# First-layer edge sums split around the row maxima, with one block difference per slot

## The chip, the cores and the metric

One core of a Trainium2 chip runs the kernel. The metric is the device time of one execution in microseconds (us), taken as the median of several runs. A core has five engines that run side by side: TensorE (PE, with its weight load PEld), VectorE (DVE), ScalarE (ACT), GpSimd (POOL) and SyncE (SP), which issues the DMA transfers here. Each engine works through its own queue in order and waits on semaphores for the others.

## The reference, cut to what matters

There are two layers; the change is in the first one, a graph attention over 8 batches (B) of 512 tokens with 512 features (F). The second is a normal self-attention with 16 heads and is not touched.

```python
self_feat = concat(x, q) @ W_self.T + b_self            # B x 512 x 512
for d in range(2):                                       # adjacency and its transpose
    A = adj if d == 0 else swapaxes(adj, 1, 2)
    A = A[:, :, :20, :]                                  # 20 neighbours, 11 labels
    cond = A.sum(-1)                                     # sum over the 11 labels
    vb = A @ w_bias + b_bias                             # weighted sum over the labels
    aff = einsum(q_heads, k_heads) / sqrt(dh)
    aff = where(cond > 0, aff, -9e15) + vb
    w = softmax(aff)                                     # over the 20 neighbours
    output += attention(w, kv, Wout) + bout
x = x + relu(output)
```

For each token there are 16 heads x 40 scores (2 directions x 20 neighbours), 640 numbers in a row. The mask and the additive term depend on token and neighbour only: 40 numbers per token, made from 440 integer labels.

## The kernel before, in words

A batch is called a block `b`. It is cut into four pieces `c` of 128 tokens, so the first layer has 32 slots `n` = 4b + c, written out as one Python loop under a manual schedule: the order of the statements in the loop is the order of each engine's queue. In slot n the loop works on several pieces at once:

- `turn_weights(n)` (L561) turns the finished softmax weights on PE, and ACT copies them out (L563).
- `normalize0(n+1)`: ACT takes the exponential (L550), DVE sums it and takes the reciprocal (`den`, L553 and L554), and POOL multiplies by it (L555).
- `scores0(n+2)`: PE makes the scores (`pss`, L529), DVE takes them out of PSUM (L533) and POOL multiplies by the mask (L535).
- `add_edges(n+2)`: POOL adds the additive term (L539).
- `self_feat_product`: PE makes a later block's features by a seven-product scheme for 2x2 quarters (L356). Per block, the slots c = 0 to 3 carry the products (4, 5), (3), (1, 2) and (6, 7); DVE or ACT takes them out, and DVE adds the collected ones at the slot's end (`TO_ADD0`, L692: none at c = 0 and 1, one at c = 2, three at c = 3).
- `result0(n)`: PE makes the output piece (`po`, L571 and L573), DVE finishes it (L574) and SP stores it.
- `less_top(n+2)`: DVE takes the row maxima (`top`, L546) and POOL subtracts them (L547).
- `edges(b+1+c//2, (c+2)%4)`: DVE makes one piece of a later block's mask and additive term in five instructions. These are a plain sum of the labels (L257), the comparison with zero that gives the mask (L258), a product with the label weights (L259), its sum (L260), and the bias (L261).
- At c = 0, DVE makes the small `lt` (L292) for a later block; PE turns it in the next slot (`pl`, L298).
- At c = 1, `far_away(b+1)` on POOL turns the mask into 0 or -9e15 (L266) and adds it to the additive term (L267).
- At c = 1, SP also issues 20 small loads of `vo` (L516) and the two 440 KB label loads of block b+2 (L246), and before them the 1 MB load of the turned features `vt` of block b+3 (L218).
- `turned_sums(b+2, i)`: POOL makes the four quarter differences of the turned features that the products read (L342): differences 2 and 0 at c = 0, 1 at c = 1, 3 at c = 2, none at c = 3.

Some slots carry more: slots 0 and 1 the sums of the self weights (L335, DVE), slot 8 the gate vectors (L584 on DVE, `pg` on PE), slots 10 to 13 the keys of the second half on PE, and slots 15 to 18, 22 and 23 statistics and norms of the second layer's first block (L93, L111 on DVE). From slot 26 on there are no edges, differences or products. After the loop the second layer follows.

Label tiles and `vt` tiles have two buffers each, and the mask and additive tiles two each.

Of the kernel before, what the change touches and what calls it, by code (L numbers as in the profile page):

```python
# [9 lines left out]
F32 = mybir.dt.float32  # L10
# [3 lines left out]
ALU = mybir.AluOpType  # L14
AX = mybir.AxisListType
# [3 lines left out]
B, N, F = 8, 512, 512  # L19
P = 128  # L20
# [5 lines left out]
D2 = 2 * NG  # L26
# [5 lines left out]
BIG = 9000000000000000.0  # L32
# [12 lines left out]
def graph_then_self_attention(ctx: ExitStack, tc: tile.TileContext, x, x_t, near, near_t, labels, w_self_t, wq, wk_t,  # L45
                              wout_t, wg_t, wb_t, wqkv_t, wp_t, cols, gate_vecs, rows, out):
    nc = tc.nc

    def blocks(ap):
        return ap.rearrange("(c p) f -> p c f", p=P)  # L50
# [118 lines left out]
    def quarter(t, p, q):  # L169

        return t[:, 2 * p:2 * p + 2, M * q:M * (q + 1)]


    with ExitStack() as l0:
        w0 = l0.enter_context(tc.tile_pool(name="w0", bufs=1))
        two = l0.enter_context(tc.tile_pool(name="two", bufs=2))
# [32 lines left out]
        def load_x(b):  # L209
            X[b] = xp.tile([P, C, F], F32, tag="x", name=f"x_{b}")  # L210
            nc.sync.dma_start(X[b], blocks(x[b]))
# [3 lines left out]
        def load_vt(b):  # L215
            VT[b] = turned.tile([P, C, N], F32, tag="turned", name=f"vt_{b}")
            for cut in (slice(0, 2), slice(2, C)) if b == 0 else (slice(0, C),):
                nc.sync.dma_start(VT[b][:, cut], blocks(x_t[b])[:, cut])  # L218
# [21 lines left out]

        MASK, ADD, LABELS = {}, {}, {}

        def load_labels(b):
            for i in range(2):
                LABELS[b, i] = two.tile([P, 2, D2 * L], I32, tag="labels", name=f"labels_{b}_{i}")
                nc.sync.dma_start(LABELS[b, i], labels[b, i * N // 2:(i + 1) * N // 2, :].rearrange("(c p) m -> p c m", p=P))  # L246

        def edges(b, c):


            if c == 0:
                MASK[b] = two.tile([P, C, D2], F32, tag="mask", name=f"mask_{b}")
                ADD[b] = two.tile([P, C, D2], F32, tag="add", name=f"add_{b}")
            src = LABELS[b, c // 2][:, c % 2, :].rearrange("p (m l) -> p m l", l=L)
            weighted = src.bitcast(F32)
            total = two.tile([P, D2], F32, tag="total", name=f"total_{b}_{c}")
            nc.vector.tensor_reduce(total, src, AX.X, ALU.add)  # L257
            nc.vector.tensor_scalar(MASK[b][:, c, :], total, 0.0, None, ALU.is_gt)  # L258
            nc.vector.tensor_tensor(weighted, src, edge_bc[:, None, 0:L].to_broadcast([P, D2, L]), ALU.mult)  # L259
            nc.vector.tensor_reduce(total, weighted, AX.X, ALU.add)  # L260
            nc.vector.tensor_scalar(ADD[b][:, c, :], total, edge_bc[:, L:L + 1], None, ALU.add)  # L261

        def far_away(b):

            far = two.tile([P, C, D2], F32, tag="far", bufs=1, name=f"far_{b}")
            nc.gpsimd.tensor_scalar(far, MASK[b], 1.0, BIG, ALU.subtract, ALU.mult)  # L266
            nc.gpsimd.tensor_tensor(ADD[b], ADD[b], far, ALU.add)  # L267

        vo = w0.tile([P, 2, KB, P], F32, name="vo")
        nc.gpsimd.memset(vo, 0.0)  # L270
# [48 lines left out]
        def self_feat(b, blocks_of_f):  # L319

            self_feat_rest(b, self_feat_main(b, blocks_of_f))
# [15 lines left out]
        def turned_sums(b, n):  # L337

            B11, B12, B21, B22 = (quarter(VT[b], p, q) for p in range(2) for q in range(2))
            TB[n] = {0: B12, 3: B21}.get(n) or parts.tile([P, 2, M], F32, tag=f"t{n}", name=f"ts{n + 1}_{b}")  # L340
            x0, x1 = ((B12, B11), (B22, TB.get(0)), (B22, B12), (B21, TB.get(1)))[n]
            nc.gpsimd.tensor_tensor(TB[n], x0, x1, ALU.subtract)  # L342
# [195 lines left out]
        def add_edges(b, c, engine=nc.gpsimd):  # L538
            engine.tensor_tensor(T[b, c], T[b, c], ADD[b][:, c, None].to_broadcast([P, H, D2]), ALU.add)  # L539
# [9 lines left out]
        def normalize0(b, c):  # L549
            nc.scalar.activation(T[b, c], T[b, c], AF.Exp)  # L550
            tv = T[b, c].rearrange("p h (d m) -> p (h d) m", d=2)
            den = three.tile([P, 2 * H, 1], F32, tag="den", name=f"den_{b}_{c}")
            nc.vector.tensor_reduce(den, tv, AX.X, ALU.add)  # L553
            nc.vector.reciprocal(den, den)  # L554
            nc.gpsimd.tensor_tensor(tv, tv, den.to_broadcast([P, 2 * H, NG]), ALU.mult)  # L555

        def turn_weights(b, c):
            flat = T[b, c].rearrange("p h e -> p (h e)")
            pt = pair(f"ptw_{b}_{c}").rearrange("p a n -> p (a n)")
            for i in range(KB):  # L560
                nc.tensor.transpose(pt[:, i * P:(i + 1) * P], flat[:, i * P:(i + 1) * P], ident)  # L561
            wt = two.tile([P, KB, P], F32, tag="wt", name=f"wt_{b}_{c}")
            nc.scalar.copy(wt, pt[:, :KB * P].rearrange("p (i n) -> p i n", i=KB))  # L563
            WT[b, c] = wt
# [33 lines left out]
        for n in range(2 * C):  # L598
            d, f = n % 2, n // 2
# [20 lines left out]
        live_of(1)  # L620
        self_feat(1, (0, 1))
        load_vt(2)
        for n, (b, c) in enumerate(slots):
            turn_weights(b, c)

            if n + 3 == len(slots):
                scores0(*slots[n + 2])
            if n + 1 < len(slots):
                normalize0(*slots[n + 1])
            if n + 3 < len(slots):  # L630
                scores0(*slots[n + 2])
            if n + 2 < len(slots):
                add_edges(*slots[n + 2], nc.vector if n + 3 == len(slots) else nc.gpsimd)
            if n < 2:
                self_feat(1, (c + 2,))
            elif b + 1 + c // 2 < B:
                for i in ((4, 5), (3,), (1, 2), (6, 7))[c]:
                    self_feat_product(b + 1 + c // 2, i)
            if 26 <= n < len(slots) - 2:
                less_top(*slots[n + 2])  # L640
            if c == 1 and b + 2 < B:
                live_of(b + 2)
                if b + 3 < B:
                    load_vt(b + 3)
            if n in (10, 11, 12, 13):
                keys(1, n - 10, 0)
            if n in (24, 25):
                for f in (2 * (n - 24), 2 * (n - 24) + 1):
                    turn(0, f)
            group = {26: lambda: q_or_k(0, 0), 27: lambda: q_or_k(1, 0), 29: lambda: value(0), 30: lambda: value(1),  # L650
                     31: lambda: value(2)}.get(n, lambda: None)()
            if group:
                group.half(0)
                if n < 30:
                    group.half(1)
            if n == 10:
                gate_columns(gb)
            result0(b, c)
            if n >= 30:
                group.half(1)  # L660
            if n < 26:
                less_top(*slots[n + 2])
            if n in (10, 11, 12, 13):
                keys(1, n - 10, 1)
            if b + 1 + c // 2 < B:
                edges(b + 1 + c // 2, (c + 2) % 4)
            if c == 0 and b + 2 < B:
                live_sums(b + 2)
            if c == 1:
                if b + 1 < B:  # L670
                    far_away(b + 1)
                    load_vo(b + 1)
                if b + 2 < B:
                    load_labels(b + 2)
            if c == 2 and b + 2 < B:
                q_row(b + 2)
            if c == C - 1 and b + 3 < B:
                load_x(b + 3)
            if n == 4:
                WG = [weight("wg", wg_t), weight("wb", wb_t)]  # L680
            if n == 8:
                gb = gate_vectors()
                WQ.update({(d, 1): weight(f"wq{d}_1", wq[d]) for d in range(2)})

            if n < 2:
                for i in ((0, 1), (3, 2))[n]:
                    weight_sums0(i)
            if b + 2 < B:
                for i in ((2, 0), (1,), (3,), ())[c]:
                    turned_sums(b + 2, i)  # L690
            for sf, y in TO_ADD0:
                nc.vector.tensor_tensor(sf, y, sf, ALU.add)  # L692
            TO_ADD0.clear()

            if n in (17, 18, 19, 24):
                i = min(n - 17, 3)
                W1.append(weight(f"w1_{i}", (*(wqkv_t[i] for i in range(3)), wp_t)[i]))
            if n in (23, 28):
                fetch((n - 23) // 5)
            if n == 9:  # L700
                early = weight("early", mid[0])
            if 15 <= n < 19:
                norm_stats(0, n - 15, early)
            for i in {22: (0, 1), 23: (2, 3)}.get(n, ()):
                norm(0, i, early)
# [334 lines left out]
    with tc.manual_schedule():  # L1040
# [22 lines left out]
        for n, (b, g, c) in enumerate(steps):  # L1063
# [41 lines left out]
            if at in OUTPUT_SUMS_AT:  # L1105
                back, i = OUTPUT_SUMS_AT[at]
# [94 lines left out]
```

## Time and profile before

| what | value |
|---|---|
| median of 3 runs | 1327.74 us (1327.66 to 1327.84) |
| the profiled execution's own time | 1324.78 us |
| its span in the profile | 1323.0 us |
| granted TensorE clock | 0.999 |
| PE, DVE, ACT, POOL busy | 98%, 72%, 54%, 64% |
| first layer's loop of slots | about 66 us to 407 us of the span |

The profiled execution is 2.96 us (0.2%) below the median of the runs, and 1.78 us of it lie outside the span. Lines of the trace have the start in us, the duration, the engine, the line of the kernel (L555), the operation, output and inputs, and in brackets how long the engine had stood idle and what ended the wait. PE is shown as busy nearly everywhere because the ends of its pipelined matmuls are modelled, so its waits are read better from its weight loads.

### The profile page before, as it was taken

Reading aid. Unit: us, or ns where it says so; the run is one execution under the profiler, and the core shown is the slowest. Engines: PE = TensorE matmul, PEld = TensorE weight load, DVE = VectorE, ACT = ScalarE, POOL = GpSimd, SP = SyncE. Lnnn points to the kernel's source line nnn. Section 1 sums busy time; section 2 is a strip of 40 time slices with the busy share of each in tenths; the row PEclk is TensorE's granted clock in tenths of the full one; section 3 lists DMA queues with packets and bytes.
Section 4 is the critical chain, followed back from the end, with each engine's and each line's share of the span. In section 5 each row is a group of like instructions: output and inputs, shape, how many; then the busy total and the mean of one; then the engine's idle time right before and its main releaser. Section 6 shows DMA issues by size and latency. Waiting matters only on the chain.

```text
span 1323.0 us, 29745 instructions
## 1 busy us (share of the span) xinstructions
PE 1298.1 (98%) x11347; PEld 988.7 (75%) x11347; DVE 958.4 (72%) x1759; ACT 708.8 (54%) x1740; POOL 841.5 (64%) x921
## 2 busy tenths in 40 slices
PE   9999999999999999999999999999999999999997
PEld 6567777877765687777777777777777777777776
DVE  4467787777855668687768768776785876776887
ACT  2333233323225665766666666666567567566664
POOL 0066775677563546677577667756866774775776
PEclk9999999999999999999999999999999999999999
DMA  9523552343212000001002000100200010010010
GB/s 346 175 96 110 177 191 83 111 159 135 90 58 80 1 2 1 2 18 64 2 2 78 5 1 17 65 1 1 81 2 1 18 65 1 2 49 2 10 41 33
DMA packets 46492, 78.66 MB, mean 59 GB/s; under 512 B 9680, under 2 KB 14224, under 8 KB 46352
## 3 DMA queue, kind: packets, MB, share of 16 engines
q1 hardware_dynamic: 45920, 76.22, 16.7%
q8 instruction: 91, 1.49, 0.5%
q10 hardware_dynamic: 432, 0.55, 0.1%
q14 instruction: 49, 0.40, 0.1%
HBM read 59.27 MB, written 17.49 MB: 58 GB/s over the span
## 4 chain that ended last, share of the span: by engine, by line
PE 74%; DVE 13%; POOL 8%; issue 3%; ACT 1%; DMA 0%; POOLq 0%; DVEq 0%; ACTq 0%
PE pst L786 18%; PE pt L942 16%; PE s L917 9%; PE pao L957 8%; PE psp L829 6%; PE pss L529 3%; POOL t L535 3%; POOL t L539 3%; PE psf_p L356 2%; PE pqk L138 1%; DVE top L924 1%; DVE top L546 1%; DVE mask L258 1%; PE pz L124 1%; DVE den L553 1%
## 5 line engine op out<-in xcount | busy, mean ns | idle before, releaser
L937 POOL TENSOR_SCALAR e<-e,den 128x512 f32<-128x512 f32 x511 | 361.8, 708 | 267.1 <-DVE den L934 172.7
L929 ACT ACTIVATE e<-s,top 128x512 f32<-128x512 f32 x512 | 348.5, 697 | 131.5 <-DVE top L924 131.5
L924 DVE TENSOR_REDUCE top<-s 128x2 f32<-128x1024 f32 x256 | 301.0, 1217 | 18.6 <-PE s L917 17.2
L942 PEld LDWEIGHTS pt<-ident,e 128*128 128x128 f32 x2048 | 234.5, 141 | 82.4 <-POOL e L937 25.2
L942 PE MATMUL pt<-ident,e 128*128 128x128 f32 x2048 | 289.8, 276 | 3.2 <-ACT et L944 1.6
L944 ACT COPY et<-pt 128x512 f32<-128x512 f32 x369 | 209.3, 596 | 101.5 <-PE pt L942 100.7
L917 PE MATMUL s<-k_pair,q_pair 32*128 32x512 f32 x992 | 143.7, 640 | 0.0
L529 PE MATMUL pss<-kq,sf 128*128 128x320 f32 x512 | 142.9, 433 | 0.0
L957 PEld LDWEIGHTS pao<-et,v 128*32 128x32 f32 x4096 | 107.5, 110 | 44.4 <-issue 44.4
L957 PE MATMUL pao<-et,v 128*32 128x128 f32 x4096 | 126.5, 274 | 0.0
L529 PEld LDWEIGHTS pss<-kq,sf 128*128 128x128 f32 x512 | 95.0, 190 | 36.1 <-ACT kq L486 0.3
L929 ACT ACTIVATION_READ_ACCUMULATOR e<-s,top 128x1 f32 x512 | 109.2, 213 | 0.0
L944 DVE COPY et<-pt 128x512 f32<-128x512 f32 x143 | 96.3, 673 | 3.4 <-PE pt L942 2.8
L555 POOL TENSOR_TENSOR t<-t,den 128x640 f32<-128x640 f32 x32 | 40.7, 1272 | 59.6 <-DVE den L554 54.0
L550 ACT ACTIVATE t<-t 128x640 f32<-128x640 f32 x32 | 23.6, 738 | 94.0 <-POOL t L547 93.9
L535 POOL TENSOR_TENSOR t<-t,mask 128x640 f32<-128x640 f32 x32 | 49.4, 1544 | 31.2 <-issue 30.3
L546 DVE TENSOR_REDUCE top<-t 128x32 f32<-128x640 f32 x32 | 26.2, 818 | 56.3 <-POOL t L539 56.3
L547 POOL TENSOR_TENSOR t<-t,top 128x640 f32<-128x640 f32 x32 | 40.7, 1271 | 34.0 <-DVE top L546 34.0
L126 ACT ACTIVATE ht<-pz,gates_t 128x512 f32<-128x512 f32 x32 | 24.7, 777 | 64.6 <-PE pz L124 64.6
L563 ACT COPY wt<-ptw 128x640 f32<-128x640 f32 x32 | 22.2, 693 | 67.4 <-PE ptw L561 67.3
L917 PEld LDWEIGHTS s<-k_pair,q_pair 32*128 32x128 f32 x992 | 41.0, 183 | 20.8 <-issue 17.3
L786 PE MATMUL pst<-t,w 128*128 128x256 f32 x224 | 53.7, 383 | 0.0
(272 smaller groups left out, 2276.3 us busy)
## 6 DMA issues: line engine op xcount, KB each, us to landing
x<-in_x SPq DMA_DIRECT2D x8, 1024.0 KB
mid<-x SPq DMA_DIRECT2D x32, 256.0 KB
xq<-mid SPq DMA_DIRECT2D x8, 1024.0 KB
out<-o SPq DMA_DIRECT2D x31, 256.0 KB
vt<-in_x_t SPq DMA_DIRECT2D x7, 1024.0 KB
labels<-in_labels SPq DMA_DIRECT2D x16, 440.0 KB
wq<-in_wq SPq DMA_DIRECT2D x4, 1024.0 KB
gate<-gates SPq DMA_DIRECT2D x8, 512.0 KB
```

Of the source, the lines that this page charges most:

```text
L529: nc.tensor.matmul(o, SF[b][:, k, cut], KQ[b][:, k, on], start=(k == 0), stop=(k == C - 1))
L535: nc.gpsimd.tensor_tensor(t, t, MASK[b][:, c, None].to_broadcast([P, H, D2]), ALU.mult)
L547: nc.gpsimd.tensor_tensor(tv, tv, top.to_broadcast([P, 2 * H, NG]), ALU.subtract)
L786: nc.tensor.matmul(out[:, m, :], fixed[:, k, m * P:(m + 1) * P], moving[:, k, :], start=(k == 0), stop=(k == 1))
L829: nc.tensor.matmul(out[:, m, :], t[:, k, m * P:(m + 1) * P], a[:, k, :], start=(k == 0), stop=(k == 1))
L917: nc.tensor.matmul(S[n][j // 2][:, j % 2, :], Q[b, g][on, c * P:(c + 1) * P], K[b, g][on, :], start=True, stop=True)
L924: nc.vector.tensor_reduce(TOP[n][:, 2 * pair:2 * pair + 2], S[n][pair], AX.X, ALU.max, negate=True)
L929: nc.scalar.activation(e, S[n][pair][:, j % 2, :], AF.Exp, bias=TOP[n][:, j:j + 1], accum_out=DEN[n][:, j:j + 1])
L937: engine.tensor_scalar(E[n][j], E[n][j], DEN[n][:, j:j + 1], att_scale, ALU.mult, ALU.mult)
L942: nc.tensor.transpose(pt[:, k * P:(k + 1) * P], E[n][j][:, k * P:(k + 1) * P], ident)
L944: copy(et, pt.rearrange("p (k n) -> p k n", k=C))
L957: nc.tensor.matmul(PAO[b, g][DH * j:DH * (j + 1), at], V[b][:, k, DH * h:DH * (h + 1)], ET[n, j][:, k, :], start=(k == 0), stop=(k == C - 1))
```

## The change

`edges` gets a third argument. Its first half (label sum and mask) is now issued before `less_top` of the same slot, its second half (weighted sum and bias) after it. Before the loop, both halves of the first pieces still run together. `far_away` is on DVE instead of POOL. Each slot has one difference of turned features: 0, 1 and 3 at c = 0, 1, 2, and at c = 3 difference 2 of block b+3; one more (`turned_sums(2, 2)`) runs ahead of the loop. The first label load of block b+2 is issued at c = 0, the second stays at c = 1.

```diff
-        def load_labels(b):
-            for i in range(2):
+        def load_labels(b, halves=(0, 1)):
+            for i in halves:
...
-        def edges(b, c):
+        def edges(b, c, halves=(0, 1)):
...
+            if 0 in halves:
+                nc.vector.tensor_reduce(total, src, AX.X, ALU.add)
+                nc.vector.tensor_scalar(MASK[b][:, c, :], total, 0.0, None, ALU.is_gt)
+            if 1 not in halves:
+                return
             nc.vector.tensor_tensor(weighted, src, edge_bc[:, None, 0:L].to_broadcast([P, D2, L]), ALU.mult)
...
         def far_away(b):
...
-            nc.gpsimd.tensor_scalar(far, MASK[b], 1.0, BIG, ALU.subtract, ALU.mult)
-            nc.gpsimd.tensor_tensor(ADD[b], ADD[b], far, ALU.add)
+            nc.vector.tensor_scalar(far, MASK[b], 1.0, BIG, ALU.subtract, ALU.mult)
+            nc.vector.tensor_tensor(ADD[b], ADD[b], far, ALU.add)
...
         load_vt(2)
+        turned_sums(2, 2)
         for n, (b, c) in enumerate(slots):
...
+            if b + 1 + c // 2 < B:
+                edges(b + 1 + c // 2, (c + 2) % 4, (0,))
             if n < 26:
                 less_top(*slots[n + 2])
...
             if b + 1 + c // 2 < B:
-                edges(b + 1 + c // 2, (c + 2) % 4)
+                edges(b + 1 + c // 2, (c + 2) % 4, (1,))
...
                 if b + 2 < B:
-                    load_labels(b + 2)
+                    load_labels(b + 2, (1,))
+            if c == 0 and b + 2 < B:
+                load_labels(b + 2, (0,))
...
-            if b + 2 < B:
-                for i in ((2, 0), (1,), (3,), ())[c]:
-                    turned_sums(b + 2, i)
+            if b + 2 + c // 3 < B:
+                turned_sums(b + 2 + c // 3, (0, 1, 3, 2)[c])
```

More of the change, by code (lines that the diff above doesn't have):

```diff
@@ L241, in graph_then_self_attention @@
         MASK, ADD, LABELS = {}, {}, {}
-        def load_labels(b):
-            for i in range(2):
+        def load_labels(b, halves=(0, 1)):
+            for i in halves:
                 LABELS[b, i] = two.tile([P, 2, D2 * L], I32, tag="labels", name=f"labels_{b}_{i}")
                 nc.sync.dma_start(LABELS[b, i], labels[b, i * N // 2:(i + 1) * N // 2, :].rearrange("(c p) m -> p c m", p=P))
-        def edges(b, c):
-            if c == 0:
+        def edges(b, c, halves=(0, 1)):
+            if c == 0 and 0 in halves:
                 MASK[b] = two.tile([P, C, D2], F32, tag="mask", name=f"mask_{b}")
@@ L255, in edges @@
             weighted = src.bitcast(F32)
-            total = two.tile([P, D2], F32, tag="total", name=f"total_{b}_{c}")
-            nc.vector.tensor_reduce(total, src, AX.X, ALU.add)
-            nc.vector.tensor_scalar(MASK[b][:, c, :], total, 0.0, None, ALU.is_gt)
+            total = two.tile([P, D2], F32, tag="total", name=f"total_{b}_{c}_{halves[0]}")
+            if 0 in halves:
[3 more added lines that the diff above has]
+                return
             nc.vector.tensor_tensor(weighted, src, edge_bc[:, None, 0:L].to_broadcast([P, D2, L]), ALU.mult)
```

## The prediction

> **What bounds the kernel now.** I read the page's chain first: it tells which engine's work ended last, over the whole span.
>
> ```profile
> ## 4 chain that ended last, share of the span: by engine, by line
> PE 74%; DVE 13%; POOL 8%; issue 3%; ACT 1%; DMA 0%; POOLq 0%; DVEq 0%; ACTq 0%
> ```
>
> PE bounds most of it, but 21% is DVE and POOL. The chain in order of time puts those into the first layer's loop of slots (66 to 407 us), the stage that the change touches. So next comes the view of the line that opens each slot on PE, the turning of the weights.
>
> ```profile
> L561 PEld LDWEIGHTS ptw<-ident,t x160: 138/140/145, 76.6 to 401.4; 128*128 128x128 f32 x160
> ...
> its engine sat idle before it (us, times) until:
>   POOL t L555: 22.9, 27
> ```
>
> PE's weight load waits 22.9 us for POOL's product with `den` (L555). About a quarter us of each of the 27 waits is the modelled end of the matmul before. Comparing each slot's opening with the end of its predecessor's output (L573), what PE really loses is 8.0 us in slots 2 to 9 and 7.4 us in slots 16 to 25. Slots 10 to 15 have none: the second keys fill PE. These 15.4 us are about the most that the change can win.
>
> What L555 waits for is seen in the timeline of one slot (c = 0, slot 20), from one L555 to the next:
>
> ```profile
> 305.40 1.27 POOL L555 TENSOR_TENSOR t<-t,den 128x640 f32<-128x640 f32 x1 [4.55 <-DVE den L554]
> ...
> 308.26 1.54 POOL L539 TENSOR_TENSOR t<-t,add 128x640 f32<-128x640 f32 x1
> ...
> 309.83 0.82 DVE L546 TENSOR_REDUCE top<-t 128x32 f32<-128x640 f32 x1 [1.45 <-POOL t L539]
> 310.57 0.60 DVE L257 TENSOR_REDUCE total<-labels 128x40 f32<-128x440 int32 x1
> 310.74 1.27 POOL L547 TENSOR_TENSOR t<-t,top 128x640 f32<-128x640 f32 x1 [0.94 <-DVE top L546]
> 311.21 0.84 DVE L258 TENSOR_SCALAR mask<-total 128x40 f32<-128x40 f32 x1
> ...
> 311.97 1.74 POOL L342 TENSOR_TENSOR ts<-vt 128x512 f32<-128x512 f32 x1
> 311.97 0.60 DVE L259 TENSOR_TENSOR labels<-labels,vec 128x440 f32<-128x440 int32 x1
> 312.04 0.74 ACT L550 ACTIVATE t<-t 128x640 f32<-128x640 f32 x1 [3.76 <-POOL t L547]
> 312.60 0.61 DVE L260 TENSOR_REDUCE total<-labels 128x40 f32<-128x440 f32 x1
> 313.25 0.49 DVE L261 TENSOR_SCALAR add<-total,vec 128x40 f32<-128x40 f32 x1
> ...
> 313.73 0.80 DVE L553 TENSOR_REDUCE den<-t 128x32 f32<-128x640 f32 x1
> ...
> 315.07 1.27 POOL L555 TENSOR_TENSOR t<-t,den 128x640 f32<-128x640 f32 x1
> ```
>
> The reader sees a ring: L555, L535, L539, then `top` 4.43 us after L555's start, L547, the exponential (done at 312.78), `den`, and 1.34 us later L555 again. `den` could have started at about 312.8; it started at 313.73, because DVE was at the edges. With no edges the ring takes 8.74 us (slot 26). Also, DVE stood idle for 1.45 us just before `top`.
>
> Two rows behave oddly. L258 takes 0.84 us here and 0.18 at its shortest, and it ends as POOL's L547 ends (312.01 against 312.05). L342 takes 1.74 us beside L259, and 1.27 elsewhere. Such DVE and POOL instructions exclude each other. Who goes first is seen at slot 1:
>
> ```profile
> 103.64 0.68 DVE L335 TENSOR_TENSOR s_self<-ws,s_self 128x512 f32<-128x512 f32 x1
> 103.88 0.83 POOL L267 TENSOR_TENSOR add<-add,far 128x160 f32<-128x160 f32 x1 [0.47 <-DVE add L261]
> 104.24 1.02 DVE L335 TENSOR_TENSOR ws<-ws 128x512 f32<-128x512 f32 x1
> ```
>
> L267 (0.52 alone) waits for the first L335, goes before the second, and the second ends 0.34 us late. A waiting POOL instruction gets in between two products of DVE.
>
> **The change part by part.** Times are from `top`'s start (T), in the order of DVE's queue.
>
> *First half before `top`.* L257 and L258 leave the ring: 0.60 us, and 0.76 from L258's start to L259's. They go where DVE idled. L574 at 307.71, L257 until 308.9; L258 then waits for POOL's L539 and ends with it (0.04 us later, as after L547), when `top` may start anyway. Cost 0. If PE is the bound, DVE comes late from `po` and the cover is gone: `top` is then 1.35 us after the end of `po` instead of 0.65. So POOL may run ahead of PE by about 1.4 us, no more.
>
> *Second half after `top`.* L259 now starts at T+0.74, before L547 (T+0.90). L547 is held up. Row first: L259 holds POOL off for 0.46 us of its 0.60 (slot 12: L259 at 223.65, L342 at 223.76 took 1.62, 0.35 over 1.27). So L547 runs T+1.20 to 2.47, +0.30 us on the ring. The Trainium skill ("SBUF — State Buffer", section "Who interferes with whom") states a rule against this change: a DVE operation with two SBUF inputs, and a GpSimd operation that reads SBUF, take a shared port pair for the whole instruction, and the later one fully blocks. By the rule's whole 0.60 us, L547 would start at T+1.34: +0.44. That would be 0.14 us more in each of some 18 slots, 2.5 us in all; I take the row. L261 ends with L547, at T+2.5. The exponential ends at T+3.24, `den` can start, and L555 comes at T+4.60.
>
> *c = 0.* `lt` follows L261; its product on POOL comes after. Interval from L555 to L555: 4.43 + 4.60 = 9.03 us (before: 9.66). PE's 0.43 us wait for `lt` in the next slot goes too.
>
> *c = 1.* POOL loses 1.04 + 0.52 us; it was the bound here (9.94). DVE gains L266 and L267. No row shows these on DVE. The first, by L258 (40 columns, 0.18) and L111 (512 columns, 0.50): 0.26 us. The second, by L259 (440 columns, 0.60) and L335 (512, 0.68): about 0.30. Below nothing neither can be; above, each can wait for POOL's 1.27 us L342. The first follows L261 directly, as L259 follows L258, and gets in; the second needs the first's result, and in that gap the waiting L342 goes (as L267 between the L335s): T+2.75 to 4.0. The second ends at T+4.3, L555 is at T+5.6: 10.05 us. With no such wait it is 9.05.
>
> *c = 2.* L692 gets in after L261 (until T+3.0), L342 after it: 9.03 us (before 10.18).
>
> *c = 3.* Three L692 (0.60 apart), and new beside them L342. The first goes, L342 takes T+3.0 to 4.3, the others end at T+5.4: 11.18 us (before 11.14, where POOL was free). Alone they would end at T+4.3: 10.1.
>
> *What costs nothing.* The difference ahead of the loop: POOL stands idle for 6.12 us until 83.70, and `vt`, issued at 65.92, is in by about 73 (the DMA share falls to 0 from 74 us). It can delay the edges there by about 0.4 us, which slot 1's PE (bound by itself) covers. `far_away(0)` meets 2.88 us of DVE idle before 38.5. At c = 3 the new L342 reads a `vt` issued two slots earlier, with 5 us to land, and overwrites what product 7 read some 5 us before. Queues: on SP the first label load (0.4 us of issue) now stands before `vt` and the 20 `vo` issues, `vt` waits there for PE anyway; the second stays behind `vo`. Labels have at least a slot and a half to land.
>
> **The sum.** One undisturbed block before (L555 at 127.84 to 168.76) is 9.94 + 10.18 + 11.14 + 9.66 = 40.92 us. After, 39.29. PE's own need is 9.85 us for a slot with two products (233.31 to 243.12 and on), about 9.0 with one: 38.6. So the ring still binds, at c = 1 and c = 3.
>
> I walk the slots: PE opens at the later of its own need and L555 + 1.33. Slot 3 opens at 107.5 (107.85 before), 6 at 136.8 (138.82), 9 at 168.2 (170.84), 10 at 177.9 (181.60). The keys keep that 3.7 us. At slot 17 it is 3.3, since POOL's lead is capped; then 301.6 for slot 21 (306.73) and 343.9 for slot 25 (349.66). In slots 15 to 18 the statistics add 1.03 us behind the edges, and in 22 a norm waits behind L342. The gain is 5.7 us, and afterwards PE carries it to the end. The profiled execution (1324.78) would be 1319.1. The median was 2.96 higher; the same off it is 1322.0.
>
> **The rivals.**
>
> *PE becomes the bound (22%).* If DVE keeps the pair through its row of instructions at c = 1 and 3, intervals are 9.03, 9.05, 9.03, 10.1 = 37.2, under PE's 38.6. For it: L259 after L258 beats L342 every time. Against: the L335 rows. Slot 10 opens 5.8 us earlier, slots 14 to 25 bring 7.7: 13.5, so 1314.2.
>
> *POOL wins every contest (8%), slower.* If L342 takes the pair at L547's end before L261, DVE stands until T+3.8 in each slot: 9.7 + 10.1 + 10.2 + 11.45 = 41.45, 0.5 us a block over four and a half blocks, plus 0.7 at the statistics of c = 1: about 3 us, 1330.7. It decides where L261 is longer than 1.5 us. Against: in all the slots before, L258 waiting behind L547 went ahead of L342.
>
> *It is given back (12%).* The lead cap or another DVE tail takes the 0.5 to 1 us a slot back, and PE's waits move to `po` or products: 1326 to 1328. For it: a quarter of the ring's freed time already goes to L547.
>
> **How the numbers follow.** My forecast has 58%, and its own range is 1319 to 1324.7 (the 2.5 us of the rule, the two contests each way). With the others: 80% faster, 12% within 0.2% (2.7 us, about what a measurement of this kernel can tell from no change), 8% slower. The range 1315 to 1327 leaves out the fastest end and the slower case.
>
> **What would show it.** Right: L258 ends with L539 and `top` does not move from L555 + 4.43; L547 starts 1.2 us after `top`; L555's wait of PE falls from 22.9 to about 17 us; c = 2 drops to 9.0; at c = 3 an L692 of about 1.3 us more. Wrong: `top` later than 4.6 us after L555 outside the keys' slots, L261 over 1.5 us, POOL waiting for `vt`, or PE waiting for products.

## The result and the profile after

The changed kernel takes 1318.0 us (median of 4 runs, 1315.49 to 1318.51), the kernel before, run beside it, 1327.7. The ratio is 0.9926, with a 95% interval of 0.9909 to 0.9943: it is faster by 0.7%, or 9.7 us. The profiled execution took 1315.49 us with a span of 1313.7, 9.3 us less than the one before, at the same granted clock of 0.999.

The page's chain shows where DVE and POOL have gone: their 21% have become 10%, and PE's 74% have become 87%.

```profile
## 4 chain that ended last, share of the span: by engine, by line
PE 87%; DVE 8%; POOL 2%; issue 1%; ACT 1%; DMA 0%; POOLq 0%; DVEq 0%; ACTq 0%
```

The line that opens each slot on PE (L561 before, L564 now) waits 9.3 us instead of 22.9 for POOL's product with `den` (L558 now), and 17 times instead of 27:

```profile
L564 PEld LDWEIGHTS ptw<-ident,t x160: 138/141/144, 76.2 to 391.3; 128*128 128x128 f32 x160
...
its engine sat idle before it (us, times) until:
  POOL t L558: 9.3, 17
```

The timeline of slot 20 (c = 0), from one L558 to the next, is the counterpart of the one shown before. Lines have moved: L258 and L259 are the label sum and mask, L262 to L264 the second half, L549 the maxima, L550 their subtraction.

```profile
297.36 1.27 POOL L558 TENSOR_TENSOR t<-t,den 128x640 f32<-128x640 f32 x1 [2.41 <-DVE den L557]
...
300.22 1.54 POOL L542 TENSOR_TENSOR t<-t,add 128x640 f32<-128x640 f32 x1
300.26 0.60 DVE L258 TENSOR_REDUCE total<-labels 128x40 f32<-128x440 int32 x1
300.90 0.90 DVE L259 TENSOR_SCALAR mask<-total 128x40 f32<-128x40 f32 x1
301.79 0.82 DVE L549 TENSOR_REDUCE top<-t 128x32 f32<-128x640 f32 x1
302.53 0.61 DVE L262 TENSOR_TENSOR labels<-labels,vec 128x440 f32<-128x440 int32 x1
302.69 1.58 POOL L550 TENSOR_TENSOR t<-t,top 128x640 f32<-128x640 f32 x1 [0.93 <-DVE top L549]
303.17 0.61 DVE L263 TENSOR_REDUCE total<-labels 128x40 f32<-128x440 f32 x1
303.81 0.49 DVE L264 TENSOR_SCALAR add<-total,vec 128x40 f32<-128x40 f32 x1
304.22 0.16 DVE L295 TENSOR_SCALAR lt<-sums 128x4 f32<-128x4 f32 x1
304.23 1.29 POOL L345 TENSOR_TENSOR vt<-vt 128x512 f32<-128x512 f32 x1
304.30 0.74 ACT L553 ACTIVATE t<-t 128x640 f32<-128x640 f32 x1 [4.06 <-POOL t L550]
305.07 0.82 DVE L556 TENSOR_REDUCE den<-t 128x32 f32<-128x640 f32 x1 [0.69 <-ACT t L553]
...
306.42 1.27 POOL L558 TENSOR_TENSOR t<-t,den 128x640 f32<-128x640 f32 x1 [0.91 <-DVE den L557]
```

The mask, held up by POOL's addition, ends with it (301.80 against 301.76), and the maxima start 4.43 us after L558 as before. The subtraction (L550) starts 0.90 us after the maxima as before and takes 1.58 us instead of 1.27: what the prediction had as a later start shows in the profile as a longer instruction. `den` now waits for ACT, where it used to wait for DVE's row of edge work: 0.69 us of DVE idle stand before it. The interval is 9.06 us instead of 9.67.

Intervals from one POOL product with `den` to the next, by the c of the slot that they start in (slots 4 to 7 of before and after; PE's own need is 9.8 us for a slot with two products and 8.5 for one with one):

| c | before | predicted | measured |
|---|---|---|---|
| 0 | 9.66 | 9.03 | 9.07 |
| 1 | 9.94 | 10.05 | 9.66 |
| 2 | 10.18 | 9.03 | 9.06 |
| 3 | 11.14 | 11.18 | 11.08 |
| sum | 40.92 | 39.29 | 38.87 |

The contests of c = 1 and c = 3, in which DVE and POOL want to run instructions that exclude each other, are seen in the timeline: first slot 21, then slot 19, and last slot 19 of the kernel before. L269 and L270 are the large number on DVE, L699 (L692 before) the collected sums, L345 POOL's difference:

```profile
312.88 0.49 DVE L264 TENSOR_SCALAR add<-total,vec 128x40 f32<-128x40 f32 x1
313.29 0.23 DVE L269 TENSOR_SCALAR far<-mask 128x160 f32<-128x160 f32 x1
313.29 1.36 POOL L345 TENSOR_TENSOR ts<-vt 128x512 f32<-128x512 f32 x1
313.36 0.74 ACT L553 ACTIVATE t<-t 128x640 f32<-128x640 f32 x1 [4.07 <-POOL t L550]
313.55 1.28 DVE L270 TENSOR_TENSOR add<-add,far 128x160 f32<-128x160 f32 x1
...
314.75 0.81 DVE L556 TENSOR_REDUCE den<-t 128x32 f32<-128x640 f32 x1
```

```profile
293.14 2.96 DVE L699 TENSOR_TENSOR sf<-ys,sf 128x512 f32<-128x512 f32 x3
293.14 1.80 POOL L345 TENSOR_TENSOR ts<-vt 128x512 f32<-128x512 f32 x1
```

```profile
302.25 1.89 DVE L692 TENSOR_TENSOR sf<-ys,sf 128x512 f32<-128x512 f32 x3
```

L270 takes 1.28 us, and 0.33 where POOL is free (its minimum is 0.326): it ends 0.18 us after L345 (314.83 against 314.65). The three L699 take 2.96 us instead of 1.89, and L345 1.80 instead of 1.27, as one L699 goes before it and two after it.

### The profile page after: what moved, and what is told of

It is laid out like the page before. It is cut to its first block, busy times and chain, and to the rows that moved or that the text cites. A ratio compares the mean times of both kernels' runs of the same rounds, so it can differ in the third digit from the quotient of the medians.

```text
span 1313.7 us, 29713 instructions
## 1 busy us (share of the span) xinstructions
PE 1295.4 (99%) x11347; PEld 988.2 (75%) x11347; DVE 974.7 (74%) x1775; ACT 710.1 (54%) x1740; POOL 842.1 (64%) x905
## 4 chain that ended last, share of the span: by engine, by line
PE 87%; DVE 8%; POOL 2%; issue 1%; ACT 1%; DMA 0%; POOLq 0%; DVEq 0%; ACTq 0%
PE pst L793 19%; PE pt L949 17%; PE s L924 10%; PE pss L532 8%; PE pao L964 8%; PE psp L836 6%; PE psf_p L359 4%; PE psf L312 2%; PE po L576 2%; PE pqk L138 2%; DVE top L931 2%; PE pz L124 1%; PE ptw L564 1%; PE pw L501 1%; PE pq L482 1%
## 5 line engine op out<-in xcount | busy, mean ns | idle before, releaser
L944 POOL TENSOR_SCALAR e<-e,den 128x512 f32<-128x512 f32 x511 | 366.8, 718 | 262.4 <-DVE den L941 168.5
L558 POOL TENSOR_TENSOR t<-t,den 128x640 f32<-128x640 f32 x32 | 40.7, 1273 | 54.9 <-DVE den L557 54.3
L553 ACT ACTIVATE t<-t 128x640 f32<-128x640 f32 x32 | 23.6, 738 | 91.5 <-POOL t L550 91.5
L550 POOL TENSOR_TENSOR t<-t,top 128x640 f32<-128x640 f32 x32 | 47.4, 1480 | 38.9 <-DVE top L549 38.9
L851 DVE TENSOR_TENSOR xq<-psp,xq 128x512 f32<-128x512 f32 x30 | 20.2, 689 | 45.9 <-PE psp L836 40.7
```

The costliest lines, as they stand in the source:

```text
L944: engine.tensor_scalar(E[n][j], E[n][j], DEN[n][:, j:j + 1], att_scale, ALU.mult, ALU.mult)
```

## The experiments

Two measures are used. One is the time as a ratio to the kernel before. The other is read from the profiles, from PE's opening of slot 3 to that of slot 29. It leaves out what happens ahead of the loop, which differs between executions: slot 0 opened between 75.7 and 78.4 us in the profiles below. It is 277.8 us before and 269.05 in the changed kernel. The kernel before was run beside each group of runs; its median there was 1326.1, 1325.6 and 1325.4 us instead of 1327.7, so times of different groups are better compared by their ratios.

The first four runs take single parts of the change alone or out. Theory A is that of the prediction: a ring of POOL, DVE and ACT limits a slot, and the DVE and POOL instructions exclude each other. Rival B is that the relief of POOL brings the gain.

**Split only.** The other parts are at their old places.

```diff
-            nc.vector.tensor_scalar(far, MASK[b], 1.0, BIG, ALU.subtract, ALU.mult)
-            nc.vector.tensor_tensor(ADD[b], ADD[b], far, ALU.add)
+            nc.gpsimd.tensor_scalar(far, MASK[b], 1.0, BIG, ALU.subtract, ALU.mult)
+            nc.gpsimd.tensor_tensor(ADD[b], ADD[b], far, ALU.add)
...
-                    load_labels(b + 2, (1,))
-            if c == 0 and b + 2 < B:
-                load_labels(b + 2, (0,))
+                    load_labels(b + 2)
...
-        turned_sums(2, 2)
...
-            if b + 2 + c // 3 < B:
-                turned_sums(b + 2 + c // 3, (0, 1, 3, 2)[c])
+            if b + 2 < B:
+                for i in ((2, 0), (1,), (3,), ())[c]:
+                    turned_sums(b + 2, i)
```

> Only the split of the edge sums around the maxima is kept; the large number is on POOL again, and the differences and label loads are at their old slots. Theory A (a ring POOL, DVE, ACT limits a slot, and DVE and POOL instructions that use two SBUF operands exclude each other): intervals from one L555 product to the next of about 9.5 (c = 0: two differences on POOL, the second delays the product), 9.8 (c = 1: POOL again does the large number and a difference), 9.05 (c = 2) and 10.05 us (c = 3: no difference beside the three sums): 38.4 against 38.9 of the changed kernel. PE's need of about 38 us is then nearly the bound, so the time is that of the changed kernel or slightly less, 1317 to 1319 us. Rival B (the gain comes from relieving POOL: fewer instructions there and one difference a slot): most of the gain is gone, 1323 us or more.

Measured: 1315.0 us, ratio 0.9917 (0.9904 to 0.9930), 2 us under the range that was expected, of which 1.6 are the lower median of the kernel before. Intervals are 9.47, 9.54 and 10.0 us at c = 0, 1 and 3 (9.8 was expected at c = 1), and slot 3 to 29 takes 267.6 us. The split alone brings the whole gain. Rival B falls: POOL had all of its old work here. But at c = 2 the interval is 9.31 us in slot 2, 10.70 in slot 6 and 11.58 in slot 22 (which has a norm; 10.67 in the changed kernel), over the expected 9.05. The view of the label sum's line says why:

```profile
L258 DVE TENSOR_REDUCE total<-labels x32: 596/602/612, 27.6 to 350.1; 128x40 f32<-128x440 int32 x32
its engine sat idle before it (us, times) until:
  DMA labels<-in_labels: 7.7, 6
```

DVE now asks for the labels before the maxima, and their load, issued behind the 20 small ones, is not in yet. In the changed kernel no wait stands in this view. So the moved load has a use that the expectation had not seen; two further runs, told last, take it up.

**No split.** The rest of the change, with the edge sums in one piece after the maxima.

```diff
-            if b + 1 + c // 2 < B:
-                edges(b + 1 + c // 2, (c + 2) % 4, (0,))
...
-                edges(b + 1 + c // 2, (c + 2) % 4, (1,))
+                edges(b + 1 + c // 2, (c + 2) % 4)
```

> The changed kernel with the edge sums in one piece after the maxima again; the large number on DVE, one difference a slot and the label loads stay. Theory A: intervals of 9.66, 10.15, 10.2 and 11.15 us, sum 41.2 against 40.9 before: no gain, 1327 to 1330 us. Rival B (relieving POOL is what helps): a good part of the gain stays, 1320 to 1323 us.

Measured: 1329.6 us, ratio 1.0022 (1.0016 to 1.0028), slower by 0.2%. Rival B falls here too. Intervals are 9.66, 10.08, 10.19 and 11.39 us; slot 3 to 29 takes 281.7 us. So without the split the other parts cost 3.9 us there. Of these, 2.6 are in slot 24 alone (14.82 us, 12.22 before), where PE waits for DVE and then runs at a lower clock; this is shown in the last section.

**Old differences.** The changed kernel with POOL's differences at their old slots (the `turned_sums` lines of the first diff, and none ahead of the loop).

> The changed kernel with the differences of turned features at their old slots (2 and 0 at c = 0, none at c = 3), and none ahead of the loop. Theory A: at c = 3 the three sums of DVE no longer contend with a POOL difference, 10.05 instead of 11.08 us; at c = 0 POOL's second difference delays its product to about 9.5 instead of 9.06. Sum 38.3 against 38.9, near PE's own need of about 38: 0.5 to 2 us faster than the changed kernel, 1316 to 1317.5 us. Rival B: spreading the differences is part of the gain, and without it the time rises to 1320 us or more.

Measured: 1314.0 us, ratio 0.9906 (0.9892 to 0.9920), again 2 us under the range that was expected. The interval at c = 3 falls from 11.08 to 10.01 us, that at c = 0 rises from 9.06 to 9.47, the others stay. Slot 3 to 29 takes 267.2 us, 1.85 less than the changed kernel. The difference that was moved to c = 3 cost there what the contest with the three sums takes, as A says.

**Large number on POOL.** The changed kernel with `far_away` on POOL (the first lines of the first diff).

> The changed kernel with the large number on POOL again. Theory A: at c = 1 POOL does it (about 1.6 us with its wait) ahead of the difference, so its product is ready at about 9.8 instead of 9.66 us; nothing else moves: within 1 us of the changed kernel, 1318 to 1319 us. Rival B: POOL's 1.6 us a block come back in full at c = 1, 11.2 us, eight times less what PE covers: 1322 us or more.

Measured: 1313.7 us, ratio 0.9904 (0.9890 to 0.9917). The interval at c = 1 is 9.52 us, less than 9.66 and not the 9.8 that I had expected; slot 3 to 29 takes 268.2 us, 0.8 less than the changed kernel. DVE's wait for POOL's difference at c = 1 costs slightly more than POOL's own two instructions did. Most of the 0.8 us is in slot 17, where statistics follow: its interval is 10.05 us instead of 10.67. Of the 4 us by which the time is under the expected 1318, 1.6 are the lower median of the kernel before beside these runs, 0.8 are in the loop, and 0.45 are ahead of it, as slot 3 opened that much earlier than in the changed kernel's profile. The rest was not separated.

**The changed kernel again**, as the measure of the three runs told after it:

> The changed kernel once more, beside the others of this call, as their measure. Both theories: about 0.7% below the kernel before, and from the opening of slot 0 to that of slot 29 on TensorE about 299.4 us, as in its first profile (309.0 before).

Measured: 1316.6 us, ratio 0.9932 (0.9920 to 0.9945). Slot 0 to 29 takes 300.2 us, 0.9 over the first profile, all of it before slot 3: POOL's first product came 8.3 us after slot 0's opening instead of 7.4. Slot 3 to 29 takes 269.09 us, 0.04 from the first. By this one repeat, that measure is sound to a tenth of a us or so, and the times to about 2 us. So of the 9.7 us that slots 0 to 29 gained in the first profile, 0.9 came ahead of slot 3 and did not come again.

**No product.** It takes away the suspected cause of the longer subtraction.

```diff
-            nc.vector.tensor_tensor(weighted, src, edge_bc[:, None, 0:L].to_broadcast([P, D2, L]), ALU.mult)
-            nc.vector.tensor_reduce(total, weighted, AX.X, ALU.add)
+            if 0 in halves:
+                nc.vector.tensor_tensor(weighted, src, edge_bc[:, None, 0:L].to_broadcast([P, D2, L]), ALU.mult)
+                nc.vector.tensor_reduce(total, weighted, AX.X, ALU.add)
+            else:
+                nc.vector.tensor_reduce(total, src, AX.X, ALU.add)
```

> The changed kernel with the product with the label weights left out in the loop of slots: the second half sums the plain labels, so the additive term of all blocks but the first ones is another. Theory A (the product's two operands exclude POOL's subtraction of the maxima for 0.3 us): that subtraction takes 1.27 us instead of 1.58, and the intervals from one L555 product to the next at c = 0 and 2 fall from 9.06 to about 8.75 us, the bare ring; c = 1 and c = 3 fall by 0.3 to 0.6 us. Time within 2 us of the changed kernel, as PE needs its 9.8 us in most slots. Rival C (POOL's subtraction is slower for another reason, the neighbouring sums): 1.58 us stays.

The view of the subtraction's line (L553 in this kernel, minimum, median and maximum in ns):

```profile
L553 POOL TENSOR_TENSOR t<-t,top x32: 1262/1271/1274, 71.5 to 383.6; 128x640 f32<-128x640 f32 x32
```

All 32 take 1.27 us; in the changed kernel the median is 1.573. The intervals at c = 0 and 2 are 8.77, at c = 1 9.35 and at c = 3 10.77 us, each 0.3 less. So the product holds POOL off for 0.30 us on the ring, the size that the prediction took from the row. Rival C falls. The only run took 1312.6 us, 4 us under the changed kernel where no more than 2 were expected, and slot 3 to 29 takes 265.2 us: the product costs the changed kernel 3.9 us there.

**Edges ahead.** Both halves before the maxima, to ask whether any use of DVE's idle time there would do.

```diff
-                edges(b + 1 + c // 2, (c + 2) % 4, (0,))
+                edges(b + 1 + c // 2, (c + 2) % 4)
...
-            if b + 1 + c // 2 < B:
-                edges(b + 1 + c // 2, (c + 2) % 4, (1,))
```

> The changed kernel with both halves of the edge sums ahead of the maxima, none after. Theory A: the mask ends with POOL's addition as now, but the product, its sum and the bias then stand between the addition and the maxima on the ring, 1.4 us: maxima about 5.8 us after L555's start instead of 4.43, intervals of about 10.1 us at c = 0 and 2 and about 11 at c = 3; sum about 42 us, 1328 to 1334 us. Rival D (any order that uses DVE's idle time before the maxima wins, because DVE's row after the maxima is what binds): intervals of about 9 us and a time at or below the changed kernel's.

Measured: 1327.2 us, ratio 1.0015 (1.0007 to 1.0023). The timeline of slot 20:

```profile
308.12 1.27 POOL L558 TENSOR_TENSOR t<-t,den 128x640 f32<-128x640 f32 x1 [1.81 <-DVE den L557]
...
310.97 1.54 POOL L542 TENSOR_TENSOR t<-t,add 128x640 f32<-128x640 f32 x1
311.02 0.60 DVE L258 TENSOR_REDUCE total<-labels 128x40 f32<-128x440 int32 x1
311.65 0.90 DVE L259 TENSOR_SCALAR mask<-total 128x40 f32<-128x40 f32 x1
312.47 0.60 DVE L262 TENSOR_TENSOR labels<-labels,vec 128x440 f32<-128x440 int32 x1
...
313.91 0.81 DVE L549 TENSOR_REDUCE top<-t 128x32 f32<-128x640 f32 x1
```

The mask waits for POOL's addition, so what follows it starts only then, and the maxima are 5.79 us after L558 instead of 4.43. Intervals are 10.11, 9.09, 10.5 and 11.82 us. Rival D falls: the kernel is 0.15% slower than the one before. The time is slightly under the expected 1328 us; the intervals at c = 2 and 3 are 0.4 and 0.8 us over the expected ones. At c = 1 I had expected about 10 and it is 9.09, because DVE has one product less to take out there, reaches the mask earlier and gets it in before the addition.

**Folded.** A version meant to be better: no `far_away`; old differences.

```diff
                 nc.vector.tensor_scalar(MASK[b][:, c, :], total, 0.0, None, ALU.is_gt)
+                nc.vector.tensor_scalar(ADD[b][:, c, :], MASK[b][:, c, :], 1.0, BIG, ALU.subtract, ALU.mult)
...
-            nc.vector.tensor_scalar(ADD[b][:, c, :], total, edge_bc[:, L:L + 1], None, ALU.add)
+            nc.vector.scalar_tensor_tensor(ADD[b][:, c, :], total, edge_bc[:, L:L + 1], ADD[b][:, c, :], ALU.add, ALU.add)
```

> A version meant to be better: the differences at their old slots, and the large number made in each slot from the mask (128x40, in the first half, before the maxima) and added with the bias in one instruction of the second half, so that nothing more is done at c = 1. Theory A: the interval at c = 1 falls from 9.66 to about 9.1 us, as no product of DVE waits there for POOL's difference; the others as with the old differences (9.47, 9.06, 10.0): sum 37.7, below PE's need of about 38.2. From slot 0 to slot 29 about 297 us, 1 to 1.5 us less than with the old differences alone, 2 to 2.5 less than the changed kernel. Rival B (relieving POOL decides): no gain over the changed kernel, as POOL's work is that of the old differences.

Measured: 1317.0 us, ratio 0.9939 (0.9925 to 0.9952), not better than the changed kernel run again. The interval at c = 1 falls to 9.09 as expected, but that at c = 2 rises from 9.06 to 10.09; slot 3 to 29 takes 270.0 us. The timeline at c = 2 (slot 18; L544 is the subtraction, L340 the difference, L692 a collected sum):

```profile
282.81 1.57 POOL L544 TENSOR_TENSOR t<-t,top 128x640 f32<-128x640 f32 x1 [1.07 <-DVE top L543]
...
283.93 0.51 DVE L265 SCALAR_TENSOR_TENSOR add<-total,vec,add 128x40 f32<-128x40 f32 x1
284.34 1.27 POOL L340 TENSOR_TENSOR vt<-vt,ts 128x512 f32<-128x512 f32 x1
284.36 1.80 DVE L692 TENSOR_TENSOR sf<-ys,sf 128x512 f32<-128x512 f32 x1
```

With the old differences (same slot), the bias is a tensor-scalar instruction (L264), and the sum behind it goes first:

```profile
282.95 0.49 DVE L264 TENSOR_SCALAR add<-total,vec 128x40 f32<-128x40 f32 x1
283.36 0.68 DVE L699 TENSOR_TENSOR sf<-ys,sf 128x512 f32<-128x512 f32 x1
283.36 1.80 POOL L345 TENSOR_TENSOR vt<-vt,ts 128x512 f32<-128x512 f32 x1
```

The same sum wins in one case and loses 1.1 us in the other, and so in all five slots with c = 2 outside the keys. Timing does not tell the two apart: in both, the bias starts 0.45 us before the subtraction ends. The form of the bias instruction, which now reads two tiles, is the difference that stands out in these lines; no run takes it apart from the small instruction that was added ahead of the maxima, so the cause stays open.

**Old loads.** The changed kernel with both label loads at c = 1 (the `load_labels` lines of the first diff).

> The changed kernel with both label loads of a block at c = 1 again, behind the 20 small loads; nothing else is undone. In the split-only run DVE waited 7.7 us in 6 slots for labels at the first half of c = 2. Theory E (the split asks for the labels earlier, and so the moved load is needed): the same wait here, up to 2.7 us before the label sum in the c = 2 slots, whose maxima then come later than 4.43 us after POOL's product; slot 3 to 29 of 270 to 272 us instead of 269.05. Rival F (that wait came of POOL's or the large number's old places): no wait for labels, 269 us.

Measured: 1319.6 us, ratio 0.9952 (0.9939 to 0.9964); the changed kernel run again had 0.9932 (0.9920 to 0.9945). The interval of slot 6 is 10.72 us, and the view of the label sum's line shows the wait again:

```profile
L258 DVE TENSOR_REDUCE total<-labels x32: 598/602/612, 26.6 to 352.5; 128x40 f32<-128x440 int32 x32
its engine sat idle before it (us, times) until:
  DMA labels<-in_labels: 9.0, 5
```

Slot 3 to 29 takes 270.3 us, 1.2 more than in the changed kernel. Theory E holds: with the split, the labels are asked for earlier, and the earlier load is worth 1.2 us of loop. Most of the gain is there without it.

**Split and loads.** The split with the moved load; the large number on POOL and the old differences, as in the first diff without its `load_labels` lines.

> The split of the edge sums and the moved label load alone; the large number on POOL and the differences at their old slots. Theory A with E: intervals of 9.47, 9.5, 9.06 and 10.0 us, no wait for labels: slot 3 to 29 of 266 to 267 us, the shortest of all that compute the reference, and a time of 1312 to 1315 us. Rival F: no less than the split alone, 267.6 us.

Measured: 1312.3 us, ratio 0.9896 (0.9881 to 0.9912). Intervals are 9.47, 9.53, 9.06 and 10.01 us, and nothing waits for labels. Slot 3 to 29 takes 266.3 us, 2.7 less than in the changed kernel. This version beats both kernels: the interval of its ratio lies below that of the changed kernel run again, and with that of its first run it has only the ends in common (0.9912 and 0.9909). It also repeats two effects: against the old differences, the large number on DVE costs 0.86 us of loop again (0.84 in the changed kernel), and against the large number on POOL, the spread differences cost 1.88 (1.86). Against the split alone, the intervals of the ratios overlap; the loop is 1.3 us shorter.

## Why the prediction was right, and where its size was off

The direction and the cause held: 1322.0 us were forecast with a range of 1315 to 1327, and 1318.0 came out. That is 1 us under the range that the forecast's own mechanism was given (1319 to 1324.7). In slots 0 to 29 the loop gave 9.7 us where 5.7 were forecast, and 8.8 in the repeat.

- *First half before `top`, cost 0*: right, and shown by the split-only run. Outside the keys' slots the mask ends with POOL's addition or, where DVE reaches it earlier (slots 5, 17, 18 and 21), before it starts. The cap on POOL's lead is seen where a sign of being wrong was set: in slots 14 and 15, behind the keys, `top` comes 6.33 and 5.24 us after L558 (5.77 and 4.42 before). From slot 10 to 17 the kernel lost 0.37 us (0.4 forecast). That it was the cap alone is not shown: with the differences at their old slots `top` is as late there, and these slots gain 0.5 us.
- *Second half after `top`, +0.30 us*: right by the no-product run, which gives 0.30. The row was the better guide: the Trainium skill's rule on the shared port pair ("SBUF — State Buffer", "Who interferes with whom"), read with the whole shown 0.60 us, gave an estimate of 0.44.
- *c = 0, 2 and 3*: right within 0.1 us, and at c = 3 in its steps: L345 ends at T+4.24 and the last sum at T+5.39, where T+4.3 and T+5.4 were forecast.
- *c = 1*: the term that was mis-sized. I let POOL's difference start at T+2.75, after all of L269; it started at T+2.44 and took only 0.09 us more than its 1.27. It ended 0.2 us earlier than forecast, L270 0.3 us earlier, and the interval is 9.66 instead of 10.05. Slots 5, 17 and 21 have it; in slot 9 the keys that follow hide it.
- *PE's need for a slot with one product*: taken as 9.0, though the wait for `lt` was said to go. It is 8.52 us (slot 9), about 0.5 us there. The walk also let slot 10 open 0.7 us later than that need of 9.0, behind the ring; the ring's interval that starts in slot 8, with the gates, took 10.05 us, and slot 10 opened without a wait. Slot 10 thus opened 5.4 us earlier, counted from slot 0, not 3.7; 0.6 of the difference were gained ahead of slot 3 and are not there in the repeat, which is luck.
- *The end of the loop*: before, slot 28 still gave PE a wait of 0.8 us. POOL's lead has removed it, and the walk had stopped at slot 25.
- *PE's wait for L558* was forecast at 17 us and is 9.3.
- *The most that can be won*: 15.4 us was too high. The 8.0 us of slots 2 to 9 include about 2 us between slot 8's output and slot 9's opening, and there PE ran the products of the gates (`pg`, 168.96 to 170.92 us before), which stay in the changed kernel.

By stretches, the gain exceeds the walk by 1.7 us up to slot 10, by nothing up to 17, by 0.8 up to 21, by 0.6 up to 25 and by 0.9 from there to 29: the 4 us that were missing. The rival that PE becomes the bound came partly true: slots 4, 7, 8 and 10 open without any wait for POOL in both profiles, slot 3 only in the first. The rival that POOL wins every contest did not show in the changed kernel: the bias (L264) is never longer than 0.50 us. Nothing of size was given back: of the 10.1 us by which slot 29 opened earlier, 9.3 are left at the end of the span.

The experiments also show what the forecast had not weighed. The moved load was put at nothing because the labels land in time with it; whether they would without it I had not asked, and the old loads cost 1.2 us of loop. And two of the parts work against the gain: given the split, the large number on DVE costs 0.8 us of loop, and the spread differences 1.85.

## What to carry to other kernels

When a ring of engines limits a stage, ask which of an engine's instructions stand between the last arrival and the next departure, and move those that can end with a wait that exists anyway; moving all of them ahead lengthens the wait itself. Look in the trace for POOL and DVE instructions that exclude each other (here products and sums of two SBUF tiles on both engines, and DVE's mask, which has one), count them as serial, and decide for each who stands on the ring. Try each part of a change alone: here the split carried the gain, the earlier load added 1.2 us of loop to it, and the two parts that relieve POOL on paper cost time.

## What the runs showed of the hardware that was not expected

In the kernel without the split, PE waits 1.69 us for DVE in slot 24 and is then slow for 3.4 us, from 352.10 to 355.51 us at a granted clock of 0.50:

```profile
352.10 1.12 PE L574 MATMUL po<-ident,sf 128*128 128x128 f32 x4 [1.69 <-DVE sf L373]
...
353.00 2.34 PE L576 MATMUL po<-vo,wt 128*128 128x128 f32 x10
```

The ten matmuls of `po` take 2.34 us there, and 1.28 in the kernel before. The windows around the wait, with busy time of PE, PEld, DVE, ACT and POOL and then the granted TensorE clock:

```profile
348.00:352.00 4.00, 1.95 (x11) 1.16 (x10) 3.96 (x10) 1.45 (x2) 1.15 (x1) 1.00 0.10 36
352.00:356.00 4.00, 3.90 (x20) 3.91 (x21) 1.85 (x5) 0.00 (x0) 3.15 (x3) 0.57 0.01 2
```

With the edges ahead, slot 24 has a wait of 1.69 us too, and the clock is 0.72 from 350 to 356 us. Where the slow clock follows, a slot loses more than the wait: slot 24 took 2.6 us more than before, where its wait was 0.43 us. But the wait alone does not bring the slow clock. The kernel before has one of 1.97 us ahead of slot 10, in a stretch in which PE is about as little busy, and the clock stays at 1.00:

```profile
178.00:182.00 4.00, 2.03 (x19) 1.84 (x18) 3.93 (x8) 0.59 (x1) 2.13 (x3) 1.00 1.03 357
182.00:186.00 4.00, 4.00 (x19) 2.89 (x18) 1.36 (x3) 0.69 (x1) 2.99 (x3) 1.00 0.40 135
```

What makes the difference, no run here shows. The page's row of 40 slices does not show the slow stretch.
